# Layer 1 of a two-layer graph network: the sums over neighbours from two float32r parts of the input instead of three bf16 parts

## The chip, the cores and the metric

The kernel runs on one core of one Trainium2 chip. A core has five engines with a queue of instructions each: TensorE (matrix products, PE in the profile, with its weight loads as PEld), VectorE (DVE), ScalarE (ACT), GpSimd (POOL) and SyncE (SP), beside 16 DMA engines that move data between the chip's main memory (DRAM) and the on-chip memory. The metric is device time in microseconds: the median of three runs is 3812.68 us, and the runs lie between 3807.86 and 3813.3.

## The reference, cut to what matters

There are 16 graphs of N = 1024 nodes with F = 256 features, and a 0/1 adjacency matrix for each. Two attention layers follow each other. Layer 0 has one head; layer 1, which the change concerns, has four:

```python
# x: (16, 1024, 256), adj: (16, 1024, 1024) of zeros and ones
# layer 1 is called with adj as the mask AND as adj_seq
bias_mat = -1000000000.0 * (1.0 - adj)
coefs_adj = jax.nn.softmax(adj_seq, axis=-1)
def head(Wh, w1h, b1h, w2h, b2h, ah, bh):
    fts = inputs @ Wh
    f1, f2 = fts @ w1h + b1h, fts @ w2h + b2h
    coefs_logits = softmax(leaky_relu(f1[:, :, None] + f2[:, None, :], 0.2) + bias_mat)
    coefs = ah * coefs_logits + (1.0 - ah) * coefs_adj
    vals = coefs @ fts + bh
    return elu(vals + inputs)
# x = layernorm(x + mean over the four heads)
```

The softmax of a row of zeros and ones has only two different values, so `coefs_adj @ inputs` can be had from two sums: the sum X of all rows of the input, and the sum over the neighbours of each node, `adj @ inputs`. With deg the number of neighbours, it is (X + (e - 1) * adj @ inputs) / (N + (e - 1) * deg). The kernel computes these sums over neighbours once per graph and uses them in all four heads. They are what is changed.

## The kernel before

Everything is cut into blocks of P = 128 rows, so K = N / P = 8 and C = F / P = 2. Layer 0 writes the transposed mask of each graph to DRAM as bf16 (`mt_dram`), and layer 1 reads it back into `mt`, [128, 8, 1024]. bf16 holds zeros and ones exactly. The input x in float32 is not exact in bf16, so it is split into three bf16 parts whose sum is x:

```python
        def split(self, k):

            if k == 0:
                self.xs = pk.tile([P, K, 3, F1], BF16, tag="xs", name=f"xs_{self.b}", bufs=1)
                nc.vector.memset(self.xs[:, :, 0, F:F1], 1.0)
            xk = self.x[:, k, :]
            d = pk.tile([P, F], F32, tag="d", name=f"d_{self.b}_{k}", bufs=2)
            nc.scalar.copy(self.xs[:, k, 0, 0:F], xk)                                      # L659
            nc.vector.tensor_tensor(d, xk, self.xs[:, k, 0, 0:F], ALU.subtract)            # L660
            nc.scalar.copy(self.xs[:, k, 1, 0:F], d)                                       # L661
            nc.vector.tensor_tensor(self.xs[:, k, 2, 0:F], d, self.xs[:, k, 1, 0:F], ALU.subtract)  # L662
```

The sums of one block of 128 rows are then 24 products into one PSUM tile: 8 blocks k of the contraction times 3 parts. A column of ones beside the first part gives deg.

```python
        def neighbours(self, it):

            b = self.b
            pm = ps_s.tile([P, F1], F32, tag="s", name=f"pm_{b}_{it}")
            for k in range(K):
                lhsT = self.mt[:, k, it * P : (it + 1) * P]
                for part in (0, 1, 2) if k < K - 1 else (1, 2, 0):
                    n = F1 if part == 0 else F
                    nc.tensor.matmul(                                                       # L685
                        pm[:, 0:n], lhsT, self.xs[:, k, part, 0:n],
                        start=(k == 0 and part == 0), stop=(k == K - 1 and part == 0),
                    )
            ...
            nc.vector.scalar_tensor_tensor(                                                 # L691
                self.S[it // 2][:, it % 2], pm[:, 0:F], E1, self.X, ALU.mult, ALU.add
            )
            nc.scalar.copy(self.deg[:, it : it + 1], pm[:, F:F1])                           # L694
```

The main work of layer 1 is the attention of each head. For each block of rows (a "slot"), `gather` multiplies the weights w with the values g (pu, 8 products in plain float32), `mix` adds the share of S, `turn` transposes the result (pt), and `linear` multiplies with the head's weight (pv). The mask is used there too, by VectorE, still as bf16:

```python
            nc.vector.scalar_tensor_tensor(                                                 # L741
                w, self.A[h][:, half], self.ce[:, 0, k, h : h + 1], self.mt[:, k, half],
                ALU.max, ALU.mult,
            )
        ...
                nc.tensor.matmul(                                                           # L760
                    self.pu, w[:, self.t * P : (self.t + 1) * P], self.g.g[self.h][:, k, :],
                    start=(k == 0), stop=(k == K - 1),
                )
```

The preparation of graph b + 1 is spread over the 32 slots of graph b: its steps are hung onto slot numbers. For the first graph they run in the same order with little beside them.

```python
        for k in range(K):
            steps[18 + k // 2].append(lambda k=k: g.split(k))
        steps[22].append(g.total)
        for it in range(K):
            steps[24 + it].append(lambda it=it: g.neighbours(it))
        steps[31].append(g.shares)
```

Two places in layer 0 serve as yardsticks below. The divisors multiply float32 weights with one column, 8 products per graph, and the values of layer 0 go to DRAM from GpSimd's queue, as 1024 runs of 1 KB:

```python
                for it in range(K):                                        # divisors
                    nc.tensor.matmul(                                      # L436
                        pd[:, it : it + 1], sm[b][:, it * P : (it + 1) * P], ones[:, 0:1],
                        start=True, stop=True,
                    )
                ...
                nc.gpsimd.dma_start(wh_dram[b], wx[:, :, 0:F])             # L175
```

Of the kernel before, what the change touches and what calls it, by code (L numbers as in the profile page):

```python
# [7 lines left out]

F32 = mybir.dt.float32
BF16 = mybir.dt.bfloat16  # L10
AF = mybir.ActivationFunctionType
ALU = mybir.AluOpType
AX = mybir.AxisListType
# [2 lines left out]
P = 128  # L16
# [7 lines left out]
def kernel(  # L24
# [29 lines left out]
    nc = tc.nc  # L54
    B, N, F = x.shape
    H = W.shape[0]
    K = N // P
# [12 lines left out]
    vecs = cpool.tile([P, P], F32, name="vecs")  # L70
    ident16 = cpool.tile([P, P], BF16, name="ident16")
    nc.vector.tensor_copy(ident16, ident)
# [3 lines left out]
    wh_dram = [dpool.tile([P, K, F], F32, name=f"wh_dram_{b}") for b in range(B)]  # L76
    mt_dram = [dpool.tile([P, K, N], BF16, name=f"mt_dram_{b}") for b in range(B)]

# [6 lines left out]
    with ExitStack() as l0:  # L85
# [14 lines left out]
        F2 = F + 2  # L100
        with tc.tile_pool(name="apool", bufs=1) as apool, tc.tile_pool(
            name="aps", bufs=2, space=PSUM
# [13 lines left out]
            for name, v in (  # L116
# [3 lines left out]
                n = v.shape[0] // P  # L120
# [59 lines left out]
        with tc.tile_pool(name="bpool", bufs=1) as bpool, tc.tile_pool(  # L180
            name="bps", bufs=2, space=PSUM
# [77 lines left out]
            KV = 5  # L259
            powers = bpool.tile([P, B, K, 8], BF16, name="powers")  # L260
            nc.vector.memset(powers, 1.0)
# [13 lines left out]
            for b in range(B):  # L275
# [11 lines left out]
                for it in range(K):  # L287
                    d = bpool.tile([P, N], BF16, tag="d", name=f"d_{b}_{it}", bufs=2 * K)
                    if it < KV:
# [3 lines left out]
                    else:  # L293
                        nc.scalar.activation(
                            d, th, AF.Sign, bias=ec[:, b, it : it + 1], scale=-1.0
                        )
# [69 lines left out]
        with tc.tile_pool(name="wk", bufs=1) as wk, tc.tile_pool(  # L366
            name="ps_a", bufs=4, space=PSUM
        ) as ps_a, tc.tile_pool(name="ps_t", bufs=2, space=PSUM) as ps_t, tc.tile_pool(
            name="ps_s", bufs=2, space=PSUM
# [26 lines left out]
            def rows_in(b, it):  # L396
                rows_of[b, it] = wk.tile([P, N], BF16, tag="mr", name=f"mr_{b}_{it}", bufs=4)
                nc.gpsimd.dma_start(rows_of[b, it], adj[b, it * P : (it + 1) * P, :])

            def mask(b, it):  # L400

                if it == 0:
                    mts[b] = wk.tile([P, K, N], BF16, tag="mt", name=f"mt0_{b}", bufs=2)
                pt = ps_t.tile([P, K, P], BF16, tag="t", name=f"ptm_{b}_{it}")
                for k in range(K):
                    nc.tensor.transpose(  # L406
                        pt[:, k, :], rows_of[b, it][:, k * P : (k + 1) * P], ident16
                    )
                nc.vector.tensor_copy(mts[b][:, :, it * P : (it + 1) * P], pt)
                if it == K - 1:  # L410
                    nc.sync.dma_start(mt_dram[b], mts[b])

            def weights(b, k):

                e = wk.tile([P, N], F32, tag="e", name=f"e_{b}_{k}", bufs=3)
                nc.scalar.activation(  # L416
                    e, ebs[b], AF.Prelu, bias=c1[:, k, b : b + 1], scale=s1[:, k : k + 1],
                    alpha=SLOPE,
                )
                nc.scalar.activation(  # L420
                    e, e, AF.Exp, bias=v2[:, k : k + 1], scale=u2[:, k : k + 1]
                )
# [53 lines left out]
            for b in (0, 1):  # L476
                load(b)
                for it in range(K):
                    n = b * K + it + 4
# [7 lines left out]
            for b in range(B):  # L487
                for n in range(NH * K):
                    hf, k = divmod(n, K)
# [7 lines left out]
                    if n % 2 == 1 and b + 2 < B:  # L497
                        it = n // 2
# [60 lines left out]
    pk = ctx.enter_context(tc.tile_pool(name="pk", bufs=1))  # L559
# [3 lines left out]
    ps_f = ctx.enter_context(tc.tile_pool(name="ps_f", bufs=1, space=PSUM))  # L563
    ps_s = ctx.enter_context(tc.tile_pool(name="ps_s", bufs=2, space=PSUM))

    F1 = F + 1

    class Graph:


        def __init__(self, b):
            self.b = b
            self.A, self.g, self.w = {}, {}, {}
            self.S, self.acc = {}, {}

        def load(self):
            b = self.b
# [8 lines left out]
        def elu(self, oc):  # L586
# [3 lines left out]
            nc.scalar.activation(  # L590
                m, hv, AF.Exp, bias=t3[:, oc : oc + 1], scale=s3[:, oc : oc + 1]
            )
# [44 lines left out]
        def factors(self):  # L637
# [7 lines left out]
            f2 = self.f[:, :, H : 2 * H]  # L645
            nc.scalar.activation(self.ce[:, 0], f2, AF.Exp, scale=SLOPE - 1.0)
            nc.scalar.activation(self.ce[:, 1], f2, AF.Exp)
            nc.vector.tensor_tensor(
# [3 lines left out]
        def split(self, k):  # L652

            if k == 0:
                self.xs = pk.tile([P, K, 3, F1], BF16, tag="xs", name=f"xs_{self.b}", bufs=1)
                nc.vector.memset(self.xs[:, :, 0, F:F1], 1.0)
            xk = self.x[:, k, :]
            d = pk.tile([P, F], F32, tag="d", name=f"d_{self.b}_{k}", bufs=2)
            nc.scalar.copy(self.xs[:, k, 0, 0:F], xk)  # L659
            nc.vector.tensor_tensor(d, xk, self.xs[:, k, 0, 0:F], ALU.subtract)  # L660
            nc.scalar.copy(self.xs[:, k, 1, 0:F], d)  # L661
            nc.vector.tensor_tensor(self.xs[:, k, 2, 0:F], d, self.xs[:, k, 1, 0:F], ALU.subtract)  # L662

        def total(self):

# [8 lines left out]
            nc.scalar.copy(self.X, px)  # L674
            self.deg = pk.tile([P, K], F32, tag="deg", name=f"deg_{b}", bufs=2)

        def neighbours(self, it):

            b = self.b
            pm = ps_s.tile([P, F1], F32, tag="s", name=f"pm_{b}_{it}")  # L680
            for k in range(K):
                lhsT = self.mt[:, k, it * P : (it + 1) * P]
                for part in (0, 1, 2) if k < K - 1 else (1, 2, 0):
                    n = F1 if part == 0 else F
                    nc.tensor.matmul(  # L685
                        pm[:, 0:n], lhsT, self.xs[:, k, part, 0:n],
                        start=(k == 0 and part == 0), stop=(k == K - 1 and part == 0),
                    )
            if it % 2 == 0:
                self.S[it // 2] = pk.tile([P, 2, F], F32, tag="S", name=f"S_{b}_{it}", bufs=6)  # L690
# [5 lines that stand above are left out]
# [34 lines left out]
        def values(self, h, k):  # L730

            if k == 0:
                self.g[h] = pk.tile([P, K, F1], F32, tag="g", name=f"g_{self.b}_{h}", bufs=2)
                nc.vector.tensor_copy(self.g[h][:, :, F], self.ce[:, 1, :, h])
# [97 lines left out]
    def side(g):  # L832
        steps = {n: [] for n in range(NS)}
        steps[1].append(g.load)
        for oc in range(C):
            steps[3 + oc].append(lambda oc=oc: g.elu(oc))
        for k in range(K):
            steps[5 + k].append(lambda k=k: g.residual(k))
        steps[13].append(g.norm)
        for k in range(K):  # L840
            steps[14 + k // 2].append(lambda k=k: g.logits(k))
        steps[18].append(g.factors)
        for k in range(K):
            steps[18 + k // 2].append(lambda k=k: g.split(k))
        steps[22].append(g.total)
        for it in range(K):
            steps[24 + it].append(lambda it=it: g.neighbours(it))
        steps[31].append(g.shares)
        return steps

    def head(g, h):

        steps = [[] for _ in range(KH)]
        for hf in range(NH):
            steps[hf].append(lambda hf=hf: g.rows(h, hf))
        for k in range(K):
            steps[k // 2].append(lambda k=k: g.values(h, k))
        return steps

    graphs = [Graph(b) for b in range(B)]  # L860
    first = side(graphs[0])
    for n in range(NS):
        if n == 20:
# [9 lines left out]
    for u, (g, h, hf) in enumerate(units):  # L873
        if h == 0 and hf == 0:
            following = side(graphs[g.b + 1]) if g.b + 1 < B else {}
        if hf == 0:

            nxt = units[u + 2] if u + 2 < len(units) else None
            steps = head(nxt[0], nxt[1]) if nxt else [[]] * KH
        for t in range(KH):  # L880
# [14 lines left out]
            n = (h * NH + hf) * KH + t  # L895
# [49 lines left out]
```

## Time and profile before

| | value |
|---|---|
| median of three runs | 3812.68 us |
| span of the profiled execution | 3809.4 us |
| mean granted TensorE clock | 0.974 (1.00 in the stretches of layer 1 read below) |
| L760, gather, 8192 records | 1969.1 us busy |
| L685, sums over neighbours, 3072 records | 363.5 us busy |
| L660 and L662, subtractions of the split on VectorE, 128 each | 50.3 and 51.6 us busy |
| L659 and L661, copies of the split on ScalarE, 128 each | 47.6 and 50.5 us busy |
| layer 1, first slot to the end | about 930 to 3809 us |

In the profile a line such as `L685 PE MATMUL pm<-xs,mt 128*128 128x256 bf16 x3072 | 363.5, 274 | 0.0` reads: line 685 of the kernel, engine, operation, output and inputs, the size of the array and of the moving operand, the number of instructions; then the time for which the engine was busy with the group, the mean duration of one in ns, and the idle time of the engine just before them with what ended it. Matmuls overlap, so the mean duration of one is more than what one adds to the time. A float32 product of TensorE is recorded as two passes: the 4096 products of `gather` give 8192 records. "The chain that ended last" follows the work back from the last instruction, at each step to what released it; its shares say whose time makes up the span.

### The profile page before, as it was taken

To read this page: it belongs to the slowest core of one execution; us is meant where nothing else is said; L and a number is where in the kernel's file an instruction comes from. 1 tells how busy PE (TensorE), PEld (TensorE's weight loads), DVE (VectorE), ACT (ScalarE), POOL (GpSimd) and SP (SyncE) were. 2 spreads that over 40 slices of the span, in tenths; PEclk is the share of its full clock that TensorE was granted. 3 is DMA by queue.
4 is the path that set the end of the run, shared out by engine and by line. 5 is a ranking of instruction groups with operands and counts; after the bars stand their busy time and mean duration, and the time that the engine had idled before them with its cause. 6 is when DMAs were issued, how large, how long until landed. Compare 5 with 4: busy or idle time off the path is not lost.

```text
span 3809.4 us, 52614 instructions
## 1 busy us (share of the span) xinstructions
PE 3666.2 (96%) x20401; PEld 2979.0 (78%) x20401; DVE 2780.2 (73%) x6260; ACT 1491.1 (39%) x2977; POOL 195.8 (5%) x249
## 2 busy tenths in 40 slices
PE   8878999995999999999999999999999999999998
PEld 6664555554888888888888888888888888888887
DVE  3377877855778777877777777877787778777766
ACT  1176655632434343424343433434343424243332
POOL 0001111100000000000000000000000000000000
PEclk9958999996999999999999999999999999999999
DMA  7317766733010101000010000000101010000000
GB/s 228 129 39 168 190 181 163 192 119 127 12 45 12 45 12 45 33 24 34 23 37 31 26 31 29 28 31 26 45 12 45 12 45 34 23 34 23 4 9 12
DMA packets 87513, 224.40 MB, mean 59 GB/s; under 512 B 5688, under 2 KB 56160, under 8 KB 77024
## 3 DMA queue, kind: packets, MB, share of 16 engines
q1 hardware_dynamic: 64128, 170.41, 12.3%
q0 software_dynamic: 22784, 50.34, 6.8%
q8 instruction: 162, 2.65, 0.3%
q14 instruction: 87, 0.71, 0.1%
q10 hardware_dynamic: 352, 0.28, 0.0%
HBM read 170.68 MB, written 83.89 MB: 67 GB/s over the span
## 4 chain that ended last, share of the span: by engine, by line
PE 86%; DVE 8%; issue 3%; DMA 2%; POOL 1%; ACT 1%; SPq 0%; ACTq 0%; POOLq 0%; DVEq 0%
PE pu L760 42%; PE pa L451 11%; PE pv L785 10%; PE pm L685 9%; PE pw L170 3%; PE pt L779 3%; DVE w L741 2%; PE pf L633 1%; PE pA L723 1%; PE ptm L406 1%; DMA mr<-in_adj_dram 1%; PE px L629 1%; POOL rs L82 1%; PE pd L436 1%; DVE s L773 1%
## 5 line engine op out<-in xcount | busy, mean ns | idle before, releaser
L760 PE MATMUL pu<-g,w 128*128 128x257 f32 x8192 | 1969.1, 380 | 0.0
L760 PEld LDWEIGHTS pu<-g,w 128*128 128x128 f32 x8192 | 1481.3, 190 | 176.5
L741 DVE SCALAR_TENSOR_TENSOR w<-A,ce,mt 128x512 f32<-128x512 f32 x1024 | 738.6, 738 | 2.6 <-PE pu L760 2.6
L785 PE MATMUL pv<-W1s,sT 128*128 128x256 f32 x2048 | 525.2, 379 | 0.5 <-ACT sT L781 0.5
L451 PE MATMUL pa<-em,wh 128*128 128x512 f32 x1024 | 475.0, 605 | 0.0
L781 ACT COPY sT<-pt 128x256 f32<-128x256 f32 x512 | 190.0, 371 | 681.9 <-PE pt L779 681.2
L785 PEld LDWEIGHTS pv<-W1s,sT 128*128 128x128 f32 x2048 | 385.3, 189 | 58.5 <-ACT sT L781 3.1
L685 PE MATMUL pm<-xs,mt 128*128 128x256 bf16 (+1 forms) x3072 | 363.5, 274 | 0.0
L771 DVE TENSOR_SCALAR z<-pu 128x1 f32<-128x1 f32 x512 | 78.5, 153 | 376.8 <-PE pu L760 374.6
L800 ACT ACTIVATE m<-v,neg 128x512 f32<-128x512 f32 x256 | 184.5, 721 | 415.9 <-DVE v L798 415.1
L685 PEld LDWEIGHTS <-mt 128*128 128x128 bf16 x3072 | 301.3, 98 | 53.0 <-issue 0.3
L451 PEld LDWEIGHTS pa<-em,wh 128*128 128x128 f32 x1024 | 185.6, 192 | 180.1 <-issue 179.1
L769 ACT ACTIVATE s<-S,q 128x256 f32<-128x256 f32 x512 | 257.8, 509 | 21.9 <-DVE q L712 21.9
L773 DVE SCALAR_TENSOR_TENSOR s<-pu,z,s 128x256 f32<-128x256 f32 x512 | 245.4, 479 | 14.0 <-ACT s L769 4.0
L735 ACT ACTIVATE g<-x,ce 128x256 f32<-128x256 f32 x512 | 213.5, 497 | 62.4 <-PE pu L760 62.4
L779 PE MATMUL pt<-ident,s 128*128 128x128 f32 x1024 | 196.3, 273 | 11.5 <-DVE s L773 11.5
L779 PEld LDWEIGHTS pt<-ident,s 128*128 128x128 f32 x1024 | 141.7, 142 | 66.7 <-issue 17.5
L806 DVE SCALAR_TENSOR_TENSOR v<-m,v 128x512 f32<-128x512 f32 x192 | 132.0, 688 | 67.3 <-ACT m L800 67.3
L416 ACT ACTIVATE e<-eb,c,s 128x1024 f32<-128x1024 f32 x128 | 155.6, 1238 | 54.5 <-DVE sm L430 39.1
L798 DVE TENSOR_TENSOR v<-pv,v 128x512 f32<-128x512 f32 x256 | 176.0, 688 | 0.9 <-PE pv L785 0.9
L795 DVE TENSOR_TENSOR v<-x,bias 128x512 f32<-128x512 f32 x256 | 174.8, 683 | 1.3
L424 DVE TENSOR_TENSOR em<-e,mt 128x1024 f32<-128x1024 f32 x128 | 155.6, 1225 | 19.4 <-ACT e L420 19.4
(202 smaller groups left out, 3335.3 us busy)
## 6 DMA issues: line engine op xcount, KB each, us to landing
x<-in_x_dram SPq DMA_DIRECT2D x32, 1024.0 KB, 6.0
mr<-in_adj_dram POOLq DMA_DIRECT2D x128, 256.0 KB, 4.3
mt_dram<-mt SPq DMA_DIRECT2D x16, 2048.0 KB, 10.6
mt<-mt_dram SPq DMA_DIRECT2D x16, 2048.0 KB, 8.2
wh_dram<-wx POOLq DMA_DIRECT2D x16, 1024.0 KB, 5.0
wh<-wh_dram SPq DMA_DIRECT2D x16, 1024.0 KB, 5.2
h_dram<-hb SPq DMA_DIRECT2D x16, 1024.0 KB, 5.5
h<-h_dram SPq DMA_DIRECT2D x16, 1024.0 KB, 4.8
```

What stands on the lines that cost most here:

```text
L451: nc.tensor.matmul(acc[b, hf, oc], wh[b][:, k, oc * P : (oc + 1) * P], ems[b, k][:, hf * HALF : (hf + 1) * HALF], start=(k == 0), stop=(k ...
L685: nc.tensor.matmul(pm[:, 0:n], lhsT, self.xs[:, k, part, 0:n], start=(k == 0 and part == 0), stop=(k == K - 1 and part == 0),)
L735: nc.scalar.mul(self.g[h][:, k, 0:F], self.x[:, k, :], self.ce[:, 2, k, h : h + 1])
L741: nc.vector.scalar_tensor_tensor(w, self.A[h][:, half], self.ce[:, 0, k, h : h + 1], self.mt[:, k, half], ALU.max, ALU.mult,)
L760: nc.tensor.matmul(self.pu, w[:, self.t * P : (self.t + 1) * P], self.g.g[self.h][:, k, :], start=(k == 0), stop=(k == K - 1),)
L769: nc.scalar.mul(s, g.S[it // 2][:, it % 2], g.q[:, it, h : h + 1])
L773: nc.vector.scalar_tensor_tensor(s, self.pu[:, 0:F], z, s, ALU.mult, ALU.add)
L779: nc.tensor.transpose(pt[:, fc, :], self.s[:, fc * P : (fc + 1) * P], ident)
L781: nc.scalar.copy(self.sT, pt)
L785: nc.tensor.matmul(pv[:, self.it % 2, :], self.sT[:, fc, :], W1s[:, fc, self.h, :], start=(fc == 0), stop=(fc == C - 1),)
L798: nc.vector.tensor_tensor(v, pv, v, ALU.add)
L800: nc.scalar.activation(m, v, AF.Exp, bias=neg1, scale=1.0)
```

## The change

The input is split into two float32r numbers rather than three bf16 ones. float32r is a 32-bit format that TensorE multiplies in another way than plain float32[...]; two such parts stand for x as three of bf16 did. [...] the mask is needed as float32r too. A casting transfer from DRAM, issued by GpSimd, reads the block of the mask that `neighbours(it)` needs, three slots ahead, into one of three buffers. VectorE keeps using the bf16 mask `mt`. The row of sums has 258 columns instead of 257, so that its length is even; both extra columns hold ones. The aim is to do the sums with 16 products per block in place of 24, and the split with one subtraction and one copy per chunk in place of two and two.

```diff
-    F1 = F + 1
+    F1, F2 = F + 1, F + 2
 ...
             if k == 0:
-                self.xs = pk.tile([P, K, 3, F1], BF16, tag="xs", name=f"xs_{self.b}", bufs=1)
-                nc.vector.memset(self.xs[:, :, 0, F:F1], 1.0)
+                self.xs = pk.tile([P, K, 2, F2], F32R, tag="xs", name=f"xs_{self.b}", bufs=1)
+                nc.vector.memset(self.xs[:, :, 0, F:F2].bitcast(F32), 1.0)
             xk = self.x[:, k, :]
-            d = pk.tile([P, F], F32, tag="d", name=f"d_{self.b}_{k}", bufs=2)
             nc.scalar.copy(self.xs[:, k, 0, 0:F], xk)
-            nc.vector.tensor_tensor(d, xk, self.xs[:, k, 0, 0:F], ALU.subtract)
-            nc.scalar.copy(self.xs[:, k, 1, 0:F], d)
-            nc.vector.tensor_tensor(self.xs[:, k, 2, 0:F], d, self.xs[:, k, 1, 0:F], ALU.subtract)
+            nc.vector.tensor_tensor(
+                self.xs[:, k, 1, 0:F], xk, self.xs[:, k, 0, 0:F].bitcast(F32), ALU.subtract
+            )
 ...
+        def mask(self, it):
+
+            self.mr[it] = pk.tile([P, K, P], F32R, tag="mr", name=f"mr_{self.b}_{it}", bufs=3)
+            nc.gpsimd.dma_start(self.mr[it], mt_dram[self.b][:, :, it * P : (it + 1) * P])
+
         def neighbours(self, it):
 
             b = self.b
-            pm = ps_s.tile([P, F1], F32, tag="s", name=f"pm_{b}_{it}")
+            pm = ps_s.tile([P, F2], F32, tag="s", name=f"pm_{b}_{it}")
             for k in range(K):
-                lhsT = self.mt[:, k, it * P : (it + 1) * P]
-                for part in (0, 1, 2) if k < K - 1 else (1, 2, 0):
-                    n = F1 if part == 0 else F
+                lhsT = self.mr[it][:, k, :]
+                for part in (0, 1) if k < K - 1 else (1, 0):
+                    n = F2 if part == 0 else F
 ...
         for it in range(K):
+            steps[21 + it].append(lambda it=it: g.mask(it))
+        for it in range(K):
             steps[24 + it].append(lambda it=it: g.neighbours(it))
```

More of the change, by code (lines that the diff above doesn't have):

```diff
@@ L10 @@
 BF16 = mybir.dt.bfloat16
+F32R = mybir.dt.float32r
 AF = mybir.ActivationFunctionType
@@ L573, in __init__ @@
             self.A, self.g, self.w = {}, {}, {}
-            self.S, self.acc = {}, {}
+            self.S, self.acc, self.mr = {}, {}, {}
         def load(self):
```

## The prediction, made before the changed kernel was run

> **What bounds the kernel now.** I read the page's busy shares first, then the chain that ended last, then the groups of instructions, and last TensorE's order of time inside one slot.
>
> ```profile
> PE 3666.2 (96%) x20401; PEld 2979.0 (78%) x20401; DVE 2780.2 (73%) x6260; ACT 1491.1 (39%) x2977; POOL 195.8 (5%) x249
> ...
> PE 86%; DVE 8%; issue 3%; DMA 2%; POOL 1%; ACT 1%; SPq 0%; ACTq 0%; POOLq 0%; DVEq 0%
> PE pu L760 42%; PE pa L451 11%; PE pv L785 10%; PE pm L685 9%; PE pw L170 3%; PE pt L779 3%; DVE w L741 2%; PE pf L633 1%; PE pA L723 1%; PE ptm L406 1%; DMA mr<-in_adj_dram 1%; PE px L629 1%; POOL rs L82 1%; PE pd L436 1%; DVE s L773 1%
> ```
>
> TensorE is the bound, and the line that the change touches (L685, the sums over neighbours) is 9% of the chain: about 343 us of 3809. Now the groups that the change removes or alters:
>
> ```profile
> L685 PE MATMUL pm<-xs,mt 128*128 128x256 bf16 (+1 forms) x3072 | 363.5, 274 | 0.0
> ...
> L685 PEld LDWEIGHTS <-mt 128*128 128x128 bf16 x3072 | 301.3, 98 | 53.0 <-issue 0.3
> ```
>
> The mean of one matmul, 274 ns, is a latency: consecutive ones overlap. What one costs is the distance between starts, so I read a stretch of a middle graph in order of time (columns: start us, us, engine, line, instruction, count):
>
> ```profile
> 1612.25 1.02 PE L785 MATMUL pv<-W1s,sT 128*128 128x256 f32 x4
> 1613.11 0.60 PE L723 MATMUL pA<-ident,f 128*128 128x128 f32 x4
> 1613.55 2.84 PE L685 MATMUL pm<-xs,mt 128*128 128x257 bf16 x24
> 1616.23 1.90 PE L760 MATMUL pu<-g,w 128*128 128x257 f32 x8
> 1617.97 0.38 PE L779 MATMUL pt<-ident,s 128*128 128x128 f32 x2
> ...
> 1623.90 1.90 PE L760 MATMUL pu<-g,w 128*128 128x257 f32 x8
> ...
> 1631.14 1.90 PE L760 MATMUL pu<-g,w 128*128 128x257 f32 x8
> ```
>
> The 24 bf16 matmuls of one block of 128 rows take 1616.23 - 1613.55 = 2.68 us, 111.7 ns each for 256 or 257 columns. The 8 f32 passes of pu (4 products, each recorded as two passes) take 1617.97 - 1616.23 = 1.74 us, 217.5 ns each. So a bf16 pass takes about 0.435 ns per column and a pass of plain f32 0.846. No waiting stands between them. The busy table of the last quarter of that graph shows the same, and how much room VectorE has:
>
> ```profile
> core 0: us, PE busy (x) PEld busy (x) DVE busy (x) ACT busy (x) POOL busy (x), PEclk, DMA share, GB/s
> 1615.00:1629.50 14.50, 14.50 (x95) 12.56 (x93) 7.34 (x16) 3.92 (x10) 0.00 (x0) 1.00 0.28 119
> 1629.50:1644.00 14.50, 14.50 (x95) 12.48 (x93) 12.21 (x29) 2.62 (x8) 1.13 (x1) 1.00 0.06 19
> 1644.00:1658.50 14.50, 14.50 (x95) 12.48 (x93) 7.49 (x21) 2.21 (x7) 0.70 (x1) 1.00 0.06 19
> 1658.50:1673.00 14.50, 14.50 (x91) 12.57 (x90) 12.88 (x37) 6.61 (x17) 1.20 (x1) 1.00 0.05 18
> ```
>
> **Weight loads.** Each f32 load has a record of 190 ns but is hidden beside the 217 ns pass before it. Whether it can hide beside a pass half as long is the question. The divisors of layer 0 answer it, since there f32 weights are multiplied with a single column, so that the load alone sets the pace:
>
> ```profile
> 316.15 1.84 PE L436 MATMUL pd<-ones,sm 128*128 128x1 f32 x16
> ```
>
> Less one latency of 0.25 us, 15 intervals take 1.59 us: 106 ns per load of 128 f32 columns, with everything overlapped. The f32 transposes above agree: four of pA in 1613.55 - 1613.11 = 0.44 us, 110 ns each.
>
> **What the Trainium skill says.** "TensorE: Matmul & The Clock Gate", section "LDWEIGHTS (loading the stationary operand)", gives a load as columns over 1.2, which is 107 ns for 128; the trace's 106 agrees for f32. Its section "Weight-path perf modes — Fast Weight Load (FWL) and DoubleRow" says that loads are speeded up when there are 128 weights and the type is not FP32; the trace agrees in direction (records of 98 ns for bf16, 190 for f32). It does not say on which side float32r falls, and no page gives float32r's time per column: that is the open number here, and nothing in this trace uses the type. "DMA: Bandwidth & Descriptors", section "SWDGE vs HWDGE vs iDMA", says that a transfer that casts can only be issued from GpSimd and that one into float32r always casts; so the 128 new transfers land in GpSimd's queue, whose load is 5% now.
>
> **The change, part by part.**
> TensorE: per block, 24 bf16 matmuls become 16 float32r ones of 258 or 256 columns. The weights are loaded anew for each, now as 4-byte values. My central case is one pass per matmul at bf16's pace per column: 257 columns on average give 257 x 0.435 = 112 ns. The load needs 106 ns and fits under it, barely. I take 112 to 115, with 113: 16 x 0.113 = 1.81 us instead of 2.68, 0.87 us saved per block. There are 16 graphs x 8 blocks = 128, so 111 us. All of it lies on the path in the steady stretches, where TensorE is busy 14.50 of 14.50 us and the built program keeps the same order around the blocks.
>
> VectorE and ScalarE: each chunk of the split loses one subtraction (L660 or L662, 128 x 0.416 = 53 us) and one copy (L661, 128 x 0.407 = 52 us). Off the path except in the first graph, where nothing runs beside it: 8 x 0.416 = 3.3 us of VectorE ahead of the first sums, of which I credit 2.
>
> DMA: 128 transfers, each of 1024 runs (256 B read, 512 B written). The nearest thing in the trace is the store of wh, also 1024 runs: 0.844 us of GpSimd and 5.0 us to landing; the casting loads of adjacency rows land in 4.3. I estimate 5 us. The program issues a block's transfer when the block three earlier has been summed, some 19 us ahead at 7.24 us per slot (1623.90 to 1631.14, one pu start to the next), so it is hidden. In the first graph the sums run back to back, three buffers give only about 5 us of lead, and the program puts parts of pu between them; I charge 3 us there.
>
> VectorE's room: over the 58 us of the table it is busy 39.93. That stretch holds eight blocks and shrinks by 8 x 0.87 = 7 us, so the share goes from 69% to 78%. The fullest quarter, 12.88 of 14.5, would then be full (14.5 - 1.74 = 12.76), so I charge some lateness in handing s and w to TensorE: 0.3 us per graph, 5 us in all.
>
> Sum: -111 - 2 + 3 + 5 = -105, and 3812.7 - 105 = 3708 us, 2.8% less.
>
> **Rivals.**
> 1. float32r runs at plain f32's pace for one pass, 217 ns. Then a block takes 16 x 0.217 = 3.47 us, 0.79 more than now, 128 blocks cost +101 us: 3915. For it: the data are as wide as f32's, and TensorE may read a 4-byte column in twice the time. Two passes per matmul at bf16's pace would come out the same. Against it: splitting in two to save a third of the passes would then have no point, and the change is plainly made for that.
> 2. The weight load doesn't hide. If it adds to the stream, 106 + 112 = 218 ns, again 3915; if half of it shows, 165 ns, 2.64 us per block, and the time stays as it is. For it: load and stream are almost equal, with no slack for a handover between them. Against it: the one-column products and the transposes keep 106 to 110 ns with load and pass overlapped.
> 3. TensorE is faster, but VectorE takes over in the last quarter of each graph. It can keep at most the overhang of the fullest quarters, about 1 us per graph: 16 us more, 3724.
> 4. The casting transfers come late, because GpSimd's queue also holds the powers for the norms. A block waiting 2 us would cost 128 x 2 = 256 us; the lead of 19 us against 5 speaks strongly against it.
>
> **Range and chances.** Central mechanism with distances of 108 to 125 ns: a block saves 0.95 to 0.68 us, 128 blocks 122 to 87 us. The first without any of the charges gives 3691, the second with all of them (6 us together) 3732. Rivals 1 and 2 in full make +100 us; I give them together 13%, and distances between (above 127 ns the saving falls under 2%) 11%. The range of 8 in 10 is 3689 to 3790, leaving the heavy tail outside. Faster by over 2%: 0.76; within 2%: 0.11; slower by over 2%: 0.13.
>
> **What would show it.** In the profile after: 2048 matmuls at the line of the sums instead of 3072, a block taking 1.75 to 1.9 us from its first start to the next pu, slots of about 6.37 us instead of 7.24, VectorE near 2730 us busy and ScalarE near 1440, no wait of TensorE on the new transfers outside the first graph. 4096 matmul records, a distance near 217 ns, or idle time before the sums ended by the transfers would make the prediction wrong.

## The result, and the profile after

The changed kernel takes 3714.64 us (median of four runs, 3710.73 to 3715.75) against 3812.28 of the kernel before in the same series. The ratio is 0.9744, with a 95% interval of 0.9727 to 0.9761: 97.6 us less.

TensorE is still the bound. From the page of the changed kernel, its busy shares, the chain that ended last and the groups that answer to those shown before (now line 690 for the sums; columns as before):

```profile
PE 3571.7 (96%) x19377; PEld 2930.1 (79%) x19377; DVE 2728.9 (73%) x6132; ACT 1446.0 (39%) x2849; POOL 313.9 (8%) x377
...
PE 60%; issue 26%; DVE 8%; DMA 2%; POOL 2%; ACT 2%; SPq 0%; POOLq 0%; ACTq 0%; DVEq 0%
...
L690 PE MATMUL pm<-xs,mr 128*128 128x256 f32 (+1 forms) x2048 | 287.6, 293 | 0.3 <-DMA mr<-mt_dram 0.3
...
L690 PEld LDWEIGHTS pm<-xs,mr 128*128 128x128 f32 x2048 | 261.8, 191 | 5.7 <-issue 0.7
...
L680 POOL DMA_DIRECT2D mr<-mt_dram x128 | 118.6, 927 | 1338.6 <-PE pm L690 1321.4
```

There are 2048 matmul records for 2048 products, so a float32r product is one pass (plain f32 has two). Its weight load has a record of 191 ns, as in plain f32 (190), not of 98 as in bf16. TensorE waited 0.3 us in all for the new transfers.

The chain gives TensorE 60% and "issue" 26%, where before it gave 86% and 3%. That is not a TensorE with idle time: once per graph the chain now runs back along GpSimd through 54 us in which that engine has nothing to do, and TensorE works through them (from 1651.2 to 1705.4 us it is busy 54.20 of 54.20). The shares of this chain can't be used to weigh TensorE here.

The same place in a middle graph, in order of time:

```profile
1603.67 1.02 PE L790 MATMUL pv<-W1s,sT 128*128 128x256 f32 x4
1604.35 2.26 PE L690 MATMUL pm<-xs,mr 128*128 128x258 f32 x16
1606.44 1.90 PE L765 MATMUL pu<-g,w 128*128 128x257 f32 x8
1608.18 0.38 PE L784 MATMUL pt<-ident,s 128*128 128x128 f32 x2
1608.40 1.91 PE L765 MATMUL pu<-g,w 128*128 128x257 f32 x8
1610.14 1.02 PE L790 MATMUL pv<-W1s,sT 128*128 128x256 f32 x4
1610.82 2.27 PE L690 MATMUL pm<-xs,mr 128*128 128x258 f32 x16
1612.92 1.90 PE L765 MATMUL pu<-g,w 128*128 128x257 f32 x8
```

Here is a trap for the reader. The record of the first float32r product begins only 0.03 us after the start of the last pv pass, while that pass still runs; the second product starts 0.31 us later. The difference from one recorded pm start to the pu start, 2.09 us, is therefore too long, and the distance between pv and pm, 0.68 us, too short: four passes of pv take 0.87 us everywhere else. Counted from the true end of pv, the block takes 1606.44 - (1603.67 + 0.87) = 1.90 us. A slot takes 1612.92 - 1606.44 = 6.48 us, where it took 7.24.

To avoid the trap, all prices of a product below are worked out in one way: from the start of the last pass ahead of a block to the start of the first after it, less 216 ns for that pass, divided by the number of products; the median of 120 blocks is taken. It gives 111.6 ns before, (2894 - 216) / 24, and 119.4 after, (2126 - 216) / 16. A second clock, free of such trouble, is the time from one graph's pX to the next one's: 179.75 us before and 173.89 after.

### The profile page after: what moved, and what is told of

Same layout as the page of the kernel before. It is cut to its first block, busy times and chain, and to the rows that moved or that the text cites. A ratio compares the mean times of both kernels' runs of the same rounds, so it can differ in the third digit from the quotient of the medians.

```text
span 3714.0 us, 50585 instructions
## 1 busy us (share of the span) xinstructions
PE 3571.7 (96%) x19377; PEld 2930.1 (79%) x19377; DVE 2728.9 (73%) x6132; ACT 1446.0 (39%) x2849; POOL 313.9 (8%) x377
## 3 DMA queue, kind: packets, MB, share of 16 engines
q0 software_dynamic: 155904, 117.46, 22.6%
## 4 chain that ended last, share of the span: by engine, by line
PE 60%; issue 26%; DVE 8%; DMA 2%; POOL 2%; ACT 2%; SPq 0%; POOLq 0%; ACTq 0%; DVEq 0%
PE pu L765 26%; PE pa L452 11%; PE pv L790 6%; PE pm L690 5%; PE pw L171 3%; PE pt L784 2%; DVE w L746 2%; PE ptm L407 1%; PE pf L634 1%; DMA mr<-in_adj_dram 1%; POOL rs L83 1%; PE pA L728 1%; PE px L630 1%; PE pd L437 1%; POOL ors L83 1%
## 5 line engine op out<-in xcount | busy, mean ns | idle before, releaser
L690 PE MATMUL pm<-xs,mr 128*128 128x256 f32 (+1 forms) x2048 | 287.6, 293 | 0.3 <-DMA mr<-mt_dram 0.3
L690 PEld LDWEIGHTS pm<-xs,mr 128*128 128x128 f32 x2048 | 261.8, 191 | 5.7 <-issue 0.7
L680 POOL DMA_DIRECT2D mr<-mt_dram x128 | 118.6, 927 | 1338.6 <-PE pm L690 1321.4
L784 PE MATMUL pt<-ident,s 128*128 128x128 f32 x1024 | 196.9, 274 | 13.0 <-DVE s L778 11.4
```

Of the source, the lines that this page charges most:

```text
L690: nc.tensor.matmul(pm[:, 0:n], lhsT, self.xs[:, k, part, 0:n], start=(k == 0 and part == 0), stop=(k == K - 1 and part == 0),)
L784: nc.tensor.transpose(pt[:, fc, :], self.s[:, fc * P : (fc + 1) * P], ident)
```

## Experiments

Two things had to be told apart: what sets the price of a float32r product, and whether anything but TensorE's count of products moved the time.

**Load or stream: narrower products.** Each product is cut into two of 128 (or 130) columns.

```diff
-                    nc.tensor.matmul(
-                        pm[:, 0:n], lhsT, self.xs[:, k, part, 0:n], ...
+                    for lo, hi in ((0, P), (P, n)):
+                        nc.tensor.matmul(
+                            pm[:, lo:hi], lhsT, self.xs[:, k, part, lo:hi], ...
```

> Theory (the float32r product is paced by its weight load, about 106 ns plus a handover, 119 ns in all): halving the width and doubling the number to 32 products per block keeps 119 ns each, so a block takes 3.8 us instead of 1.91 and the kernel 3715 + 128 x 1.91 = 3959 us. Rival (paced by the stream of 256 or 258 columns, 0.465 ns per column): 32 products of 128 columns take as long as 16 of 256, 1.9 us per block, and the time stays near 3715. If float32r were slower per column for narrow rows, a block would take more than 3.8 us.

The kernel took 4007.9 us (ratio 1.0518, 1.0497 to 1.0539). One block, in order of time:

```profile
1687.11 0.60 PE L730 MATMUL pA<-ident,f 128*128 128x128 f32 x4
1687.47 3.77 PE L691 MATMUL pm<-xs,mr 128*128 128x128 f32 x32
1691.07 1.95 PE L767 MATMUL pu<-g,w 128*128 128x257 f32 x8
```

The four passes of pA take 0.44 us, so this block takes 1691.07 - (1687.11 + 0.44) = 3.52 us. The price is (3738 - 216) / 32 = 110 ns. Halving the width took only 9 ns off, so the rival's 60 ns is out, and there is a floor at 110. Every one of these products has a weight load of its own, so the load takes at most 110 ns: it is not what sets the pace of 119 at 257 columns.

That the floor is the load itself is likely, but not shown. For it: one-column products in plain f32, which have next to nothing to stream, start 111 ns apart (layer 0's divisors, read again below). Against it: 128 columns at plain f32's 0.846 ns per column also make 108 ns, and no run tells a load of 110 from a slower stream of narrow float32r products. bf16 has no such floor: in the kernel before, ten bf16 transposes of 128 columns, each with its own load, take 318.41 - 317.85 = 0.56 us, 56 ns each.

```profile
317.85 0.72 PE L406 MATMUL ptm<-ident,mr 128*128 128x128 bf16 x10
318.41 0.82 PE L383 MATMUL psrd<-ident,rc 128*128 128x128 f32 x6
```

The number of 3.8 us per block was too high, while the whole came out 49 us over the 3959 expected. Against the changed kernel it is 293 us more, of which the blocks are 128 x (3.738 - 2.126) = 206. The rest is elsewhere: TensorE waited 50.2 us for sT at pv, where the changed kernel waited 0.5.

**Load or stream: one wide product.** Both parts go through in one product of 512 columns, so there is one load for two parts. VectorE adds the halves; the numbers of neighbours are left out (a constant stands for them).

```diff
-                for part in (0, 1) if k < K - 1 else (1, 0):
-                    ... pm[:, 0:n], lhsT, self.xs[:, k, part, 0:n] ...
+                nc.tensor.matmul(
+                    pm, lhsT, self.xs[:, k].rearrange("p t f -> p (t f)"),
+                    start=(k == 0), stop=(k == K - 1),
+                )
```

> Both parts stand side by side in one product of 512 columns, 8 per block; the two halves are added by VectorE (one more operation of 0.42 us per block), and the numbers of neighbours are left out (a constant stands for them), with their column and copy. Theory (load-paced at 256 columns): the load now hides, and 512 columns at bf16's 0.435 ns take 223 ns, 1.78 us per block instead of 1.91: 3715 - 17 = 3698 us. Rival (stream-paced, 0.465 ns per column): 238 ns, 1.90 us per block, 3715. If VectorE's 53 us more were felt, the time would be above that.

Measured: 3701.66 us (0.9713, 0.9696 to 0.9729) and (2071 - 216) / 8 = 232 ns per product, between the two numbers. One block, of 1609.04 - (1606.32 + 0.86) = 1.86 us:

```profile
1606.32 1.02 PE L791 MATMUL pv<-W1s,sT 128*128 128x256 f32 x4
1607.00 2.21 PE L688 MATMUL pm<-xs,mr 128*128 128x512 f32 x8
1609.04 1.91 PE L766 MATMUL pu<-g,w 128*128 128x257 f32 x8
```

The total lies 4 us from the theory's, but the theory's reason fails with `narrow`: with the load out of the way, a column still costs (232 - 119.4) / (512 - 257) = 0.44 ns.

**The same count in bf16.** The kernel before without its third bf16 part, and with the cheaper split:

```diff
-            d = pk.tile([P, F], F32, tag="d", ...)
             nc.scalar.copy(self.xs[:, k, 0, 0:F], xk)
-            nc.vector.tensor_tensor(d, xk, self.xs[:, k, 0, 0:F], ALU.subtract)
-            nc.scalar.copy(self.xs[:, k, 1, 0:F], d)
-            nc.vector.tensor_tensor(self.xs[:, k, 2, 0:F], d, self.xs[:, k, 1, 0:F], ALU.subtract)
+            nc.vector.tensor_tensor(self.xs[:, k, 1, 0:F], xk, self.xs[:, k, 0, 0:F], ALU.subtract)
 ...
-                for part in (0, 1, 2) if k < K - 1 else (1, 2, 0):
+                for part in (0, 1) if k < K - 1 else (1, 0):
```

> The kernel before with the third bf16 part left out: 16 bf16 products per block, the split with one copy and one subtraction, no casting transfers. Theory (time follows number of products times their pace, and nothing else of the change counts): 16 x 111.7 ns = 1.79 us per block, 0.89 less than before: 3812 - 114 = 3698 us, 17 under the changed kernel. Rival (the gain of the change has another source than the count of products, for example the type): well above 3715.

Measured: 3700.15 us (0.971, 0.9696 to 0.9724), 111.8 ns per product, as in this block of 1613.58 - 1611.79 = 1.79 us:

```profile
1611.79 1.95 PE L682 MATMUL pm<-xs,mt 128*128 128x257 bf16 x16
1613.58 1.90 PE L757 MATMUL pu<-g,w 128*128 128x257 f32 x8
```

As expected: the gain of the change is that of dropping every third product, less about 15 us that the type costs.

**The same width in bf16.** The wide form with bf16 parts (edits of `wide` and `bf16_two` together; what both leave out is left out here).

> The wide form in bf16: two bf16 parts side by side, 8 products of 512 columns per block, halves added by VectorE, third part and numbers of neighbours left out, no casting transfers. Theory (a float32r column is itself dearer, 0.444 against 0.417 ns): bf16 takes 512 x 0.417 + 5 = 218 ns, a block 1.75 us against 1.87 of the wide float32r form: 3702 - 15 = 3687 us. Rival (long products of any type cost that much): 233 ns, 3702.

Measured: 3690.87 us (0.9684, 0.9668 to 0.97). One block takes 1615.46 - 1613.73 = 1.73 us, 216 ns per product:

```profile
1613.73 1.89 PE L680 MATMUL pm<-xs,mt 128*128 128x512 bf16 x8
1615.46 1.90 PE L758 MATMUL pu<-g,w 128*128 128x257 f32 x8
```

So a float32r product is 7% dearer than a bf16 one at both widths (119.4 against 111.8, 232 against 216), although at 512 columns any load of about 110 ns has long been done. The excess grows with the columns, from 8 to 16 ns, so it is not a fixed cost of each product either. It is the stream of float32r columns that is dearer. Why, no run here shows.

**A third width.** The wide form with each product cut into 384 and 128 columns.

```diff
+                for lo, hi in ((0, 384), (384, 512)):
+                    nc.tensor.matmul(pm[:, lo:hi], lhsT, xk[:, lo:hi], ...)
```

> The wide form with each product of 512 columns cut into one of 384 and one of 128 (numbers of neighbours left out as there). Theory now (a float32r product costs the larger of a load floor, 111 ns, and a stream of 5.8 ns + 0.444 ns per column, fitted to 120.0 ns at 257 columns and 233.3 at 512): 384 columns take 176 ns, 128 take 111, a block 8 x 287 = 2.30 us, 0.44 more than the wide form: 3702 + 56 = 3758 us. Rival (columns cost 0.417 ns as in bf16, and the 20 ns above 512 x 0.417 are a fixed price that at 257 columns is partly hidden): 180 ns at 384. Rival (the floor of 111 ns was an effect of two narrow products with the same weights in a row): the product of 128 columns beside a wide one takes some other time.

Measured: 3757.66 us (0.986, 0.984 to 0.9879), and (2451 - 216) / 8 = 279 ns for the pair against 287 expected. The larger of a floor and a stream holds to within 3%; as in `narrow`, the floor need not be the load's. The starts of single products in a pair (about 58 and 227 ns apart) don't give their prices, so the pair can't be cut into two numbers, and the rival's 180 ns at 384 isn't excluded by it.

**The count.** The changed kernel with the second part left out of the sums (`part in (0,)`), and with the second part multiplied twice (`(0, 1, 1)`).

> The changed kernel with the second float32r part left out of the sums: 8 products per block. Theory (119 ns for each product and nothing fixed per block): 0.955 us per block, 3715 - 122 = 3593 us. Rival (part of the 1.91 us is a fixed price for changing between plain f32 and float32r, say 0.3 us): a product would be 100 ns, a block 1.1 us, 3612.

> The changed kernel with 24 float32r products per block (the second part multiplied twice): the type at the count of the kernel before. Theory (119.8 ns each, linear in the count): a block takes 2.875 us, 0.2 more than with bf16: 3812 + 25 = 3837 us. Rival (the pace depends on the count or is shared with a fixed part): off that by more than 15 us.

Measured: 3594.15 us (0.9432, 0.9413 to 0.9451) with 8 products, 119.8 ns each; 3831.23 us (1.0051, 1.0031 to 1.0071) with 24, at 120.2 ns. The price is the same for 8, 16 and 24, so no fixed cost for changing between plain f32 and float32r shows. At equal count float32r makes the kernel slower than bf16 did. The total with 24 is 6 us under the 3837 expected.

**The cheaper split alone.** The kernel before, still with 24 bf16 products (the second part multiplied twice, the third left out), with the split of `bf16_two`.

> The kernel before with the cheaper split alone: one copy and one subtraction per chunk, still 24 bf16 products per block (the second part is multiplied twice, in place of the third, which is left out). Theory (only the products count): 3812, at most 3 us less from the first graph. Rival (VectorE's and ScalarE's 105 us of removed work were felt): clearly under 3800.

Measured: 3806.91 us against 3811.28, a ratio of 0.9989 (0.9983 to 0.9996): 4 us. The time from graph to graph is 179.59 us instead of 179.75, so some 2.6 of the 4 us come from all 16 graphs; most of that lies in the products themselves (8 x (2.894 - 2.881) = 0.10 of 0.16 us per graph), of which two in a row now stream the same part. The 105 us of work taken from VectorE and ScalarE were almost wholly beside TensorE's.

**The transfers alone.** The kernel before, with `mask` added and nothing reading its result.

> The kernel before with the 128 casting transfers added and nothing reading them. Theory (they lie beside the work): 3812, within 5 us. Rival (they take something from the other transfers or from GpSimd's powers for the norms): 10 to 30 us more.

Measured: 3815.32 us, a ratio of 1.0011 (1.0002 to 1.0019): 4 us more. With no reader to wait for, all transfers ran early, as the movement by slices shows (GB/s; the tenth to thirteenth slice):

```profile
GB/s 228 129 39 169 190 187 164 183 118 285 150 159 246 105 12 45 14 42 34 23 34 23 37 31 28 28 30 27 37 20 45 12 45 24 33 34 23 1 12 12
```

They fell together with the first graph's own loads, and pX of that graph began at 932.8 us instead of 926.2; from the third on, graphs take 179.75 us as before. In the changed kernel, where the transfers are spread, it begins at 927.1. This run therefore bounds the cost in the first graph, and not that of transfers spread as in the changed kernel. For those, compare the changed kernel with `bf16_two`, which has none: its graphs take 173.89 us against 172.88, 1.01 more, and its eight blocks 8 x (2.126 - 2.005) = 0.97 more. That leaves 0.04 us per graph for the transfers and everything else.

**The lead.** One buffer for the float32r mask instead of three (`bufs=1`).

> The changed kernel with one buffer for the float32r mask in place of three, so that a block's transfer can only start when the block before it is summed. A slot of 6.47 us less the 1.91 us of the sums leaves 4.56 us; the transfer needs 0.9 us of GpSimd's issue and 4.4 us to land, and the wait for them is felt as the difference. Theory (the lead of three buffers hides the transfers, and without it they show): 0.5 to 1 us of waiting per block, 60 to 130 us in all, 3775 to 3845. Rival (their landing doesn't matter, since the program's order or the load of other work covers it): 3715.

Measured: 3779.52 us (0.9915, 0.9896 to 0.9935), 65 us more than the changed kernel. The first graph shows the full price of a transfer without lead:

```profile
940.47 2.18 PE L690 MATMUL pm<-xs,mr 128*128 128x258 f32 x16
947.26 3.24 PE L690 MATMUL pm<-xs,mr 128*128 128x258 f32 x16 [4.62 <-DMA mr<-mt_dram]
957.05 3.77 PE L690 MATMUL pm<-xs,mr 128*128 128x258 f32 x16 [6.54 <-DMA mr<-mt_dram]
965.51 3.43 PE L690 MATMUL pm<-xs,mr 128*128 128x258 f32 x16 [4.70 <-DMA mr<-mt_dram]
973.61 3.77 PE L690 MATMUL pm<-xs,mr 128*128 128x258 f32 x16 [4.67 <-DMA mr<-mt_dram]
982.07 3.65 PE L690 MATMUL pm<-xs,mr 128*128 128x258 f32 x16 [4.69 <-DMA mr<-mt_dram]
```

In the later graphs the cost is not what was expected: 2.05 us per graph (175.94 against 173.89). About 1.1 us of it is a wait for the transfer, at one block; after that the program as built has the sums at later places in their slots, between passes of pu, and the other transfers are there in time. Much of the rest is at pt, where TensorE waited 21.3 us for s in the whole run, against 11.4 in the changed kernel.

```profile
1636.65 0.60 PE L765 MATMUL pu<-g,w 128*128 128x257 f32 x2
1638.35 2.16 PE L690 MATMUL pm<-xs,mr 128*128 128x258 f32 x16 [1.09 <-DMA mr<-mt_dram]
1640.35 1.47 PE L765 MATMUL pu<-g,w 128*128 128x257 f32 x6
```

The total is within the expected range for partly the wrong reason: about half comes from the first graph. That the lead matters is shown; 0.5 to 1 us per block is not.

**float32r at another line.** If float32r costs 120 ns where plain f32 costs 2 x 217, then three products of split operands are cheaper than one plain f32 product. `linear_split` does this to pv in the kernel before (low by low is left out); `both` does the same to `bf16_two`.

```diff
+            self.sT = pk.tile([P, 2, C, P], F32R, ...)
+            nc.scalar.copy(self.sT[:, 0], pt)
+            nc.vector.tensor_tensor(self.sT[:, 1], pt, self.sT[:, 0].bitcast(F32), ALU.subtract)
 ...
+            todo = [(0, 0, 0), (0, 1, 0), (0, 0, 1), (0, 1, 1), (1, 0, 0), (1, 1, 0)]  # part of sT, fc, part of W1
```

> The kernel before, with float32r used at another line instead: the product with the head's weight (pv), until now plain f32, from two float32r parts of each operand, in three products (high by high, high by low, low by high; low by low is left out). Per slot 4 f32 passes of 217 ns, 0.87 us, become 6 float32r products of 119.8 ns, 0.72 us. Theory (a float32r product costs its pace wherever TensorE is the bound): 512 slots x 0.15 = 76 us less, 3736 us. Rival (the split of sT puts one more VectorE operation of 0.42 us into each slot and between the transpose and pv, and TensorE waits for it): 3812 or more, with waits of TensorE on sT.

> The same, together with the sums over neighbours from two bf16 parts (the third bf16 part left out, no casting transfers). If the two savings add up, 3700 - 76 = 3624 us. If VectorE, with 213 us more to do in a shorter time, becomes felt, between 3640 and 3700.

Measured: 3753.59 us (0.9851, 0.9835 to 0.9868), and 3657.35 us (0.96, 0.9586 to 0.9614). The first gains 56 us of the 76 expected, the second 43 beyond `bf16_two`. From `both`, in order of time, with what TensorE waits for:

```profile
1606.45 0.82 PE L790 MATMUL pv<-W1r,sT 128*128 128x256 f32 x4
1607.57 0.50 PE L790 MATMUL pv<-W1r,sT 128*128 128x256 f32 x2 [0.30 <-DVE sT L785]
```

and its groups: the new VectorE operation, which starts only when ScalarE has made the high part, and the sums of waits at pv.

```profile
L790 PE MATMUL pv<-W1r,sT 128*128 128x256 f32 x3072 | 549.4, 313 | 6.1 <-DVE sT L785 5.0 <-ACT sT L784 0.5
...
L785 DVE TENSOR_TENSOR sT<-pt,sT 128x256 fp32r<-128x256 f32 x512 | 213.5, 417 | 180.4 <-ACT sT L784 178.8
```

VectorE rises to 79% of the span, and TensorE's waits for s at pt from 11.5 us before to 26.3. The mechanism carries over. A part of the gain is lost, and the waits that grew are waits for VectorE's results; that VectorE's load causes the whole loss is not shown. The changed kernel with this form of pv was not run. `both` is the fastest kernel of this study, 57 us under the changed one. It keeps less of x in the sums than three bf16 parts do.

## Why the prediction was right

The time, 3714.64 us, lies 7 us over the 3708 predicted, and inside the range. That is closer than its parts: the gain of the products was put 13 us too high, and the charges against it, 6 us in sum, came to some 1 to 3 us (98.3 us at the products, 97.6 in the medians, 95.4 in the spans). The two errors partly cancel, which is luck.

The central step, 24 products to 16 at one pass each on a path where TensorE is the bound, holds: `bf16_two`, `one_part` and `f32r_24` show that the time follows count times price, and `split_alone` that the cheaper split is worth some 4 us. That was measured beside 24 products; what the old split would cost beside 16, where VectorE has less room, was not run.

The term that was mis-sized is the price of a float32r product. The prediction put it at bf16's pace per column, "I take 112 to 115, with 113"; it measured 119.4, which is 7% over bf16. A block saves 0.768 us instead of 0.87, and 128 blocks 98 us instead of 111. The reason it gave for a price above 112, a weight load that "fits under it, barely", is wrong: by `narrow` the load takes at most 110, and `wide` against `bf16_wide` shows the same 7% where the load can't matter.

The 106 ns that the prediction read for a load in plain f32 is too low. Of the 16 loads of the divisors one was done ahead, and the other 15 follow each other without it:

```profile
316.15 1.75 PEld L436 LDWEIGHTS pd<-ones,sm 128*128 128x128 f32 x15 [0.24 <-issue]
```

Less the last record of 0.19 us, 14 intervals take 1.56 us, 111 ns each; the prediction had divided by 15 intervals, one of which no load paced. The transposes of pA at 110 ns don't confirm a load either, since their 128 columns take 108 ns at plain f32's pace. So a load in plain f32 is about as long as the stream of 112 that it was said to fit under, and the 107 of the Trainium skill ("TensorE: Matmul & The Clock Gate", section "LDWEIGHTS (loading the stationary operand)"), which the prediction found confirmed, is 4% under the 111 measured.

The sign "a block taking 1.75 to 1.9 us from its first start to the next pu" reads 2.09 in the records, because of the trap above; worked out from the pass ahead of it a block takes 1.91. Slots take 6.48 us where about 6.37 was given.

The charge for VectorE's lateness, "0.3 us per graph", was right to the tenth, though no working stood behind its size, so that the tenth is luck: eight blocks save 8 x 0.768 = 6.14 us, and a graph takes 5.86 less, so 0.28 goes back. It can be seen. TensorE begins a pt late (1.74 us is the usual distance after eight passes of pu, here it is 2.02):

```profile
1648.83 1.90 PE L765 MATMUL pu<-g,w 128*128 128x257 f32 x8
1650.85 0.41 PE L784 MATMUL pt<-ident,s 128*128 128x128 f32 x2
```

while VectorE makes the s that pt needs behind the norm of the graph's rows:

```profile
1649.11 0.75 DVE L819 BATCH_NORM_STATS2 ost<-acc 128x6 f32<-128x256 f32 x2
...
1650.21 0.48 DVE L778 SCALAR_TENSOR_TENSOR s<-pu,z,s 128x256 f32<-128x256 f32 x1
```

`bf16_two` has the same late pt (1642.64 to 1644.65, 2.01 us), with no casting transfers and no float32r, and the kernel before doesn't: it comes with the shorter blocks.

The two charges for the first graph (-2 and +3) can't be checked one by one. Together with the end of the run they are small: the spans differ by 95.4 us, of which 16 x 5.86 = 93.8 are the graphs.

Of the rivals, the first (a stream at plain f32's pace, or two passes) and the second (a load that doesn't hide) are refuted by the price itself. The third, VectorE as the new bound, cost 4 to 5 us and not 16. In the fourth, landing took 4.4 us and issue 0.93 where 5.0 and 0.84 were estimated; with the lead of three buffers nothing of it was felt, as predicted, and `mask_buf1` shows that without the lead it would have been. A wait of 2 us in every block, with which that rival was sized, did not occur in the later graphs even with one buffer; in the first graph with one buffer the waits were 4.6 to 6.5 us.

VectorE and ScalarE fell to 2729 and 1446 us busy, as predicted (2730 and 1440).

## What to carry to other kernels

When TensorE is the bound and its stretches are full, price a change as count times distance between starts, and take that distance for each type and width from full stretches, not from mean durations. On this case a float32r product of 256 columns cost 119 ns, against 112 in bf16 and 434 in plain f32: two float32r parts beat three bf16 parts, and three float32r products beat one in plain f32, but two bf16 parts are cheaper still where their precision is enough. At 128 columns a float32r product still cost 110 ns, where bf16 transposes of that width took 56: with its products cut in two this kernel was 8% slower, 206 of the 293 us by their price.

## What was not expected of the hardware

The 7% on a float32r column, at both widths, is the first surprise; its cause stays open.

The second is how much packet time the casting transfers take. The busy table of a part of a graph in the changed kernel (columns as in the table of before: the last two are the packet time as a share of the 16 DMA engines' time, and GB/s):

```profile
1592.00:1605.00 13.00, 13.00 (x79) 11.74 (x78) 7.48 (x17) 4.33 (x9) 1.99 (x2) 1.00 1.03 222
1605.00:1617.95 12.95, 12.95 (x78) 11.75 (x77) 11.48 (x29) 2.60 (x7) 2.99 (x3) 1.00 0.77 103
1617.95:1630.90 12.95, 12.95 (x78) 11.75 (x77) 7.81 (x23) 2.19 (x6) 2.51 (x3) 1.00 0.75 102
```

The share is 0.77 and 0.75 where three of the four rows of before had 0.05 to 0.06. In the first row, where other loads run too, it reads 1.03: the times of packets are added up and can exceed the engines' time, so the share is not a measure of how full the engines are. GpSimd's queue of transfers has 22.6% of 3714 us of all 16 engines after and 6.8% of 3809 before; the difference, 580 us, is 4.5 us of packet time on all engines for each of the 128 transfers. TensorE was full in all three rows, so no cost of this shows here; what it would do to a kernel that waits for its transfers, no run shows.
